# Where the constant part of an involution is added, and when a group norm takes its root

## The chip, the cores and the metric

The kernel runs on one core of a Trainium2 chip. A core has five engines with a queue of instructions each: TensorE (PE, matrix products; its weight loads are listed as PEld), VectorE (DVE), ScalarE (ACT), GpSimd (POOL) and SyncE (SP, which here issues most of the transfers). Each engine takes its own queue in order and waits on semaphores for the others. Products land in PSUM, eight banks of 2 KB per partition; all else lies in SBUF, 128 partitions wide. The metric is the time of one execution on the device, in microseconds. Before the change it is 2146.27 us, the median of three runs (2145.46 to 2147.59).

## The reference

The input `x` has 8 images, 256 channels and 56 x 56 pixels, in float32. Two layers follow each other, and the change concerns the first alone:

```python
    x = x + _L0_conv_ref(_gn(x), ...)     # layer 0: group norm, then an involution, added to x
    x = x + _L1_conv_ref(_gn(x), ...)     # layer 1: group norm, two ternary 3x3 convolutions with batch norms

    def _gn(v, G=32, eps=1e-5):
        ...
        return ((g - m) / jnp.sqrt(s + eps)).reshape(v.shape)

    def _L0_conv_ref(x, w_reduce, b_reduce, w_span, b_span):
        ker = einsum('bchw,oc->bohw', x, w_reduce) + b_reduce      # 256 -> 64 channels
        ker = einsum('bchw,oc->bohw', ker, w_span) + b_span        # 64 -> 16 groups x 49 taps
        ...
        out = (ker * patches).sum(axis=3)                          # 7x7 patches, a kernel of its own at each pixel
```

The involution makes a 7 x 7 kernel for each pixel and each of 16 groups of channels, and sums the pixel's neighbourhood with it.

## The kernel before

The program has three stages: the involution (to about 1060 us), the two convolutions, and the final sums. Only the first is changed.

**Tiling.** An image's 256 channels are taken as 4 quarters of 64 (`NCQ`, index `c`). A tile `xs[b, c]` holds one quarter of image `b`: partitions 0 to 63 the upper half of the picture, 64 to 127 the lower half, 28 rows of 56 pixels each. Each half is cut into patches of 3 x 8 pixels: 10 rows of patches (`ty`; the last has one pixel row only), 7 patches across.

**The norm is folded in.** The group norm is one scale and one shift per channel. The products use `x` as it is: the reduction's weights are scaled (`wrn`), and the sum is scaled when it is read out. What the shift adds to the involution is, per pixel, the shift times the sum of the 49 taps. This is the *constant part*.

**One row of patches**, `(b, c, ty)`, goes through these steps:

- `apply_row` (L872): 56 short products on TensorE (28 in the last row, L889) of a loaded neighbourhood `q` with the kernel matrices `a`, into a PSUM tile `pa`, of which there are two.
- `pick_out` (L893): ScalarE reads `pa` times a scale into `inv` (L899), VectorE adds the other channel groups of `pa` to it (L901), GpSimd adds `inv` to `x` (L906). In the very last quarter VectorE makes that last addition.
- `surround`, with `fill_rim` (L788, GpSimd) and `fill_end` (L801, ScalarE): they add the norm's mean at the rims of a neighbourhood that was loaded ahead.
- `generate` (L840), for the *next* quarter: 14 units. In each, TensorE makes the kernels (L857) into a pair of PSUM banks, ScalarE copies one bank with its bias into `a` (L861), VectorE the other (L865). Six banks go round between the units, the reductions and the constant part. `PER_ROW` says how many units belong to each row.
- `constant` (L810) is the last two steps of `generate`, both in row `ty` = 8. TensorE multiplies the reduced channels with the summed taps (L823, four banks). ScalarE takes each bank times the shift, plus a bias, into a tile `add` (L831), and GpSimd adds `add` to `x` of the next quarter (L837). Columns are 504 three times and 56 once.
- `reduce` (L742) and L759 make the reduced channels of the next image, in rows 24 to 34.
- One step of the rounding of the convolutions' weights (L310 to L330, VectorE, tiles `piece_w`), in most rows.
- The statistics (L149, VectorE): of the finished `x`, and of the next image's `x`.

**The norm of the next image.** `params` (L659) is a generator; from row 20 of an image on (rows counted 0 to 39 over its four quarters) it is advanced twice a row: at the start of a row, after `apply_row`, and after `pick_out`. Between two advances it emits:

1. row 20, start: a product over groups (L156); row 20, second: its read-out and the squared differences (L160 to L165);
2. row 21, start: a second product (L168); row 21, second: the variance (L171), `rstd_of` as a whole: plus epsilon (L135, VectorE), root (L137, ScalarE), reciprocal and a Newton step (L139 to L145, VectorE); then the norm's scale and shift (L173, L174), the scaled weights (L666), the scales (L673) and `shift` (L675);
3. after three empty yields, row 23, start: a product of the shift with the reduction's weights (L681); row 23, second: its read-out (L684); row 24, start: products for the rims (L688) and their copy (L692).

`gn2_params` (L695) does steps 1 and 2 for the second layer's norm, in the last image.

**Order.** After every row `pin` (L948) ties each instruction to the one before it on its engine, so every engine's queue follows the text. A long wait at the head of a queue thus holds up everything that stands behind it in the text.

Of the kernel before, what the change touches and what calls it, by code (L numbers as in the profile page):

```python
# [8 lines left out]
F32 = mybir.dt.float32  # L9
F32R = mybir.dt.float32r  # L10
AF = mybir.ActivationFunctionType
ALU = mybir.AluOpType
# [5 lines left out]
P = 128  # L18
B, C, H, W = 8, 256, 56, 56
# [70 lines left out]
def involution_tri_block_kernel(  # L90
# [37 lines left out]
    gn2 = const_tile([P, B, CT, 2], "gn2")  # L128


    def rstd_of(var, eps, name):

        n = var.shape[1]
        ve = small.tile([P, n], F32, tag=f"rs_ve{n}", name=f"ve_{name}")
        nc.vector.tensor_scalar(ve, var, eps, None, ALU.add)  # L135
        sq = small.tile([P, n], F32, tag=f"rs_sq{n}", name=f"sq_{name}")
        nc.scalar.activation(sq, ve, AF.Sqrt)  # L137
        r0 = small.tile([P, n], F32, tag=f"rs_r0{n}", name=f"r0_{name}")
        nc.vector.reciprocal(r0, sq)  # L139
        e = small.tile([P, n], F32, tag=f"rs_e{n}", name=f"e_{name}")  # L140
        nc.vector.tensor_tensor(e, r0, ve, ALU.mult)
        nc.vector.tensor_tensor(e, e, r0, ALU.mult)
        nc.vector.tensor_scalar(e, e, -0.5, 1.5, ALU.mult, ALU.add)
        r = small.tile([P, n], F32, tag=f"rs_r{n}", name=f"r_{name}")
        nc.vector.tensor_tensor(r, r0, e, ALU.mult)  # L145
        return r

    def image_stats(st, xt, j):
        nc.vector.bn_stats(st[:, j, :], xt[:, j * NC:(j + 1) * NC])  # L149
# [1 line left out]
    def group_norm_params(mv, dst, psum_tile, name, means=None):  # L151


        n = mv.shape[1]
        ps = psum_tile(f"gnp_{name}")
        nc.tensor.matmul(ps[:, :2 * n], grp_sb, mv.rearrange("p n s -> p (n s)"),  # L156
                         start=True, stop=True)
        yield
        gm = small.tile([P, n, 2], F32, tag=f"gn_gm{n}", name=f"gm_{name}")
        nc.vector.tensor_copy(gm.rearrange("p n s -> p (n s)"), ps[:, :2 * n])  # L160
        if means is not None:
            means.append(gm)
        d = small.tile([P, n], F32, tag=f"gn_d{n}", name=f"d_{name}")
        nc.vector.tensor_tensor(d, mv[:, :, 0], gm[:, :, 0], ALU.subtract)
        nc.vector.tensor_tensor(d, d, d, ALU.mult)  # L165
        yield
        ps2 = psum_tile(f"gnp2_{name}")
        nc.tensor.matmul(ps2[:, :n], grp_sb, d, start=True, stop=True)  # L168
        yield
        var = small.tile([P, n], F32, tag=f"gn_var{n}", name=f"var_{name}")  # L170
        nc.vector.tensor_tensor(var, ps2[:, :n], gm[:, :, 1], ALU.add)  # L171
        rs = rstd_of(var, GN_EPS, name)
        nc.vector.tensor_copy(dst[:, :, 0], rs)  # L173
        nc.vector.scalar_tensor_tensor(dst[:, :, 1], gm[:, :, 0], -1.0, rs, ALU.mult, ALU.mult)  # L174

    def batch_norm_before(stats, pre):

# [438 lines left out]
    with ExitStack() as ph1:  # L616
# [42 lines left out]
        def params(b):  # L659
# [13 lines left out]
                nc.vector.tensor_scalar(scales[:, c], half_sb, dst[:, c, 0:1], None, ALU.mult)  # L673
            shift = small.tile([P, NCQ], F32, tag="gn1b", name=f"gn1b_{b}")
            nc.vector.tensor_tensor(shift, dst[:, :, 1], bsum, ALU.mult)  # L675
            for _ in range(3):
                yield
            ps = ps_one(f"br_{b}")
            for c in range(NCQ):
                for i in range(2):  # L680
# [129 lines left out]
        def constant(b, c):  # L810

            n = (TY - 1) * TX
            xv = xs[b, c][:, :(TY - 1) * PY * W].rearrange("p (t y w) -> p y t w", y=PY, w=W)
            scale, bias = prm[b][0][:, c, 1:2], prm[b][2][:, c:c + 1]
            for i0 in (0, 2):
                ps = ps_pair(f"ks_{b}_{c}_{i0}")
                add = work.tile([P, 2 * PX * n], F32, tag="add", name=f"add_{b}_{c}_{i0}")
                for i in range(2):
                    py = (i0 + i) % PY
                    k0, m = (0, n) if i0 + i < PY else (NT, TX)  # L820
                    rows = slice(i * CR, (i + 1) * CR)
                    for h in range(2):
                        nc.tensor.matmul(ps[i][h * CH:(h + 1) * CH, :PX * m], wsx[rows, c, :],  # L823
                                         kr[py][rows, :, k0 + h * m:k0 + (h + 1) * m],
                                         start=True, stop=True)
                for i in range(2):
                    py = i0 + i
                    m = n if py < PY else TX
                    v = add[:, i * PX * n:i * PX * n + PX * m].rearrange(
                        "p (t w) -> p t w", w=W)  # L830
                    nc.scalar.activation(  # L831
                        v.rearrange("p t (k x) -> p t k x", x=PX),
                        ps[i][:, :PX * m].rearrange("p (x t k) -> p t k x", x=PX, k=TX),
                        AF.Identity, bias=bias, scale=scale)
                    x_ = xv[:, py] if py < PY else xs[b, c][:, PY * (TY - 1) * W:].rearrange(
                        "p (t w) -> p t w", w=W)
                    nc.gpsimd.tensor_tensor(x_, x_, v, ALU.add)  # L837
                yield

        def generate(b, c, a):  # L840
# [52 lines left out]
        def pick_out(b, c, ty, ps, n, m):  # L893
# [2 lines left out]
            inv = work.tile([P, TX, NP], F32, tag="inv", bufs=3, name=f"inv_{b}_{c}_{ty}")  # L896
            iv = inv[:, :, :n]
            scale = prm[b][1][:, c, 2 * (m == GQ):]
            nc.scalar.activation(iv, parts[:, :, 0], AF.Copy, scale=scale[:, 0:1])  # L899
            for g in range(1, m):  # L900
                nc.vector.scalar_tensor_tensor(iv, parts[:, :, g], scale[:, g:g + 1], iv,  # L901
                                               ALU.mult, ALU.add)
# [325 lines left out]
```

## Time and profile before

| | |
|---|---|
| median of three runs | 2146.27 us |
| profiled execution | 2168.06 us, of it 2166.2 us from first to last instruction |
| mean granted TensorE clock | 0.912 |
| TensorE, VectorE, ScalarE, GpSimd busy | 81%, 81%, 66%, 27% of the span |
| L831, ScalarE, 96 times 504 and 32 times 56 columns | 778 and 412 ns each |
| L837, GpSimd, the same counts | 1265 and 303 ns each |
| L901, VectorE, from PSUM, 168 and 56 columns | 377 and 272 ns each |
| L865, VectorE, from PSUM, 504 columns | 678 ns each |
| L899, ScalarE, 168 columns | 429 ns each |
| wait of the root L137 for L135 | 19.6 us in 7 times, longest 4.1 |

How to read it: a line of the profile names the source line, the engine, the operation and its tiles. "Busy" is the time in which an engine worked; idle time counts only where it sits on the way to the end. Each wait is named by what ended it; "issue" means that the profile shows nothing that the instruction waited for. TensorE's clock can be granted in part only (1.00 is full speed).

### The profile page before, as it was taken

The numbers are of one execution on the slowest core, as the hardware profiler recorded it, in microseconds if no ns is written. First come the engines' busy times: TensorE is split into PE (matmuls) and PEld (weight loads), VectorE is DVE, ScalarE is ACT, GpSimd is POOL, SyncE is SP. The second block draws the span as 40 slices with busy tenths as digits, with TensorE's granted clock in tenths as the row PEclk, the third lists the DMA queues.
The fourth block names the chain that finished last, engine by engine and source line by source line (L and its number), as shares of the span: only waits on it lengthen the run. The fifth ranks groups of instructions, "written<-read, shape, count | busy, mean of one in ns | idle before, by whom it ended". The sixth has DMA issues, their size and how long they took to land.

```text
span 2166.2 us, 70733 instructions
## 1 busy us (share of the span) xinstructions
PE 1761.7 (81%) x29680; PEld 1635.1 (75%) x29680; DVE 1756.3 (81%) x3350; ACT 1436.3 (66%) x3557; POOL 582.5 (27%) x955
## 2 busy tenths in 40 slices
PE   4898888989889898988799999998999999960000
PEld 4777777877777787776699999998999999960000
DVE  5787868787787868777799999998999999984444
ACT  3877777777878777777557666664576666653343
POOL 0564555465556546555200000000000000000000
PEclk9999999999999999999899999999999999985555
DMA  5667767686766758666733333335233333369999
GB/s 184 211 186 224 215 203 233 171 262 195 254 202 210 239 166 255 184 198 201 265 122 135 130 129 123 121 121 178 106 129 130 122 124 127 123 267 426 430 431 395
DMA packets 156250, 440.05 MB, mean 203 GB/s; under 512 B 63775, under 2 KB 74013, under 8 KB 148509
## 3 DMA queue, kind: packets, MB, share of 16 engines
q1 hardware_dynamic: 150336, 405.50, 55.0%
q10 hardware_dynamic: 5596, 30.03, 3.3%
q8 instruction: 235, 3.85, 0.8%
q14 instruction: 83, 0.67, 0.1%
HBM read 323.28 MB, written 112.20 MB: 201 GB/s over the span
## 4 chain that ended last, share of the span: by engine, by line
PE 64%; DMA 10%; DVE 10%; issue 7%; POOL 4%; ACT 3%; SPq 0%; ACTq 0%; POOLq 0%; DVEq 0%
PE c L557 40%; PE pg L857 12%; PE pa L889 7%; PE pk L750 3%; DMA y1f<-y1d 3%; DMA out_y<-x1f 2%; POOL q L788 2%; DMA y2f<-y2d 2%; ACT a L861 2%; POOL x L906 1%; PE ks L823 1%; DVE inv L901 1%; DMA x1f<-x1d 1%; DVE x1f L1140 1%; DVE a L865 1%
## 5 line engine op out<-in xcount | busy, mean ns | idle before, releaser
L557 PE MATMUL c<-pl,wq 128*128 128x392 f32 x4608 | 857.1, 348 | 9.5 <-ACT pl L429 9.2
L557 PEld LDWEIGHTS c<-pl,wq 128*128 128x128 f32 x4608 | 855.2, 190 | 11.2 <-ACT pl L429 9.6
L861 ACT ACTIVATE a<-pg,bt 126x126 f32<-126x126 f32 (+1 forms) x2048 | 530.3, 459 | 115.3 <-PE pg L857 114.8
L857 PE MATMUL pg<-kr,wl 64*126 64x140 f32 (+1 forms) x6144 | 467.9, 296 | 44.1 <-ACT a L861 16.9
L857 PEld LDWEIGHTS pg<-kr,wl 64*126 64x126 f32 x6144 | 407.6, 199 | 70.7 <-issue 26.3
L889 PE MATMUL pa<-a,q 126*32 126x48 f32 x17024 | 290.8, 215 | 68.4 <-issue 56.4
L889 PEld LDWEIGHTS pa<-a,q 126*32 126x32 f32 x17024 | 242.0, 116 | 136.2 <-issue 89.8
L865 DVE TENSOR_TENSOR a<-pg,bt 126x504 f32<-126x504 f32 (+4 forms) x640 | 281.6, 480 | 58.8 <-PE pg L857 57.3
L906 POOL TENSOR_TENSOR x<-x,inv 128x168 f32<-128x168 f32 x310 | 161.5, 521 | 413.7 <-DVE inv L901 378.9
L901 DVE SCALAR_TENSOR_TENSOR inv<-pa,gn1s,inv 128x168 f32<-128x168 f32 (+1 forms) x384 | 134.0, 351 | 160.9 <-ACT inv L899 157.8
L406 ACT CAST pl<-r 128x812 fp32r<-128x812 f32 x190 | 160.8, 867 | 131.0 <-DVE r L401 121.7
L382 POOL MEMSET xp<- 128x116 f32 x32 | 6.3, 196 | 825.6 <-DVE a L401 825.6
L788 POOL TENSOR_TENSOR q<-q,sides 126x256 f32<-126x256 f32 (+1 forms) x320 | 225.3, 705 | 6.4 <-DMA q<-in_x_nb 6.3
L407 DVE TENSOR_TENSOR pl<-r,pl 128x812 fp32r<-128x812 f32 x190 | 184.8, 998 | 25.1 <-ACT pl L406 23.5
L487 ACT ACTIVATE dummy<-y,nc 128x1568 f32<-128x1568 f32 (+1 forms) x128 | 200.2, 1564 | 4.8 <-DVE y L577 3.5
L899 ACT ACTIVATE inv<-pa,gn1s 128x168 f32<-128x168 f32 x320 | 133.2, 418 | 69.8 <-PE pa L889 48.6
L149 DVE BATCH_NORM_STATS2 st<-x 128x6 f32<-128x392 f32 x256 | 137.9, 555 | 9.8 <-DMA x<-in_x 9.4
L837 POOL TENSOR_TENSOR x<-x,add 128x504 f32<-128x504 f32 (+1 forms) x128 | 127.2, 1024 | 25.4 <-ACT add L831 25.4
L1107 ACT ACTIVATE xp<-raw,bi_bn,sc_bn 128x392 f32<-128x392 f32 (+1 forms) x125 | 83.0, 721 | 60.3 <-DVE a L401 58.9
L1087 ACT ACTIVATE xp<-raw,gn 128x392 f32<-128x392 f32 (+1 forms) x125 | 83.1, 721 | 58.9 <-DVE a L401 58.9
L1138 DVE SCALAR_TENSOR_TENSOR y1f<-y2f,sc_bn,y1f 128x3136 f32<-128x3136 f32 (+2 forms) x20 | 56.6, 2831 | 63.1 <-DMA y2f<-y2d 53.0
L750 PE MATMUL pk<-x,wrn 64*128 64x168 f32 (+1 forms) x1152 | 101.1, 315 | 0.8 <-issue 0.8
(177 smaller groups left out, 1794.9 us busy)
## 6 DMA issues: line engine op xcount, KB each, us to landing
q<-in_x_nb SPq DMA_DIRECT2D x320, 448.0 KB, 4.1
raw<-x1d SPq DMA_DIRECT2D x32, 812.0 KB, 5.9
raw<-y1d SPq DMA_DIRECT2D x32, 812.0 KB, 6.6
x<-in_x SPq DMA_DIRECT2D x64, 392.0 KB, 5.2
x1d<-x SPq DMA_DIRECT2D x64, 392.0 KB, 5.1
y1d<-y SPq DMA_DIRECT2D x30, 784.0 KB, 3.7
y2d<-y SPq DMA_DIRECT2D x30, 784.0 KB, 3.4
y1f<-y1d SPq DMA_DIRECT2D x14, 1568.0 KB, 14.2
```

Of the source, the lines that this page charges most:

```text
L406: nc.scalar.copy(hi, r)
L407: nc.vector.tensor_tensor(lo, r, hi.bitcast(F32), ALU.subtract)
L487: nc.scalar.activation(dst, v, f, bias=shift[:, to:to + 1], accum_out=stats[:, to, j, n:n + 1])
L557: nc.tensor.matmul(ps[:, to, :NM], wq[k][:, t, dx, to * P:(to + 1) * P], part[:, t, :, dx:dx + W], start=(c == 0), stop=(c == last))
L750: nc.tensor.matmul(ps[h][:, :m * W], wrn[rows, c, :], src[rows, r0:r0 + (m - 1) * PY + 1:PY, :], start=(c == 0), stop=(c == NCQ - 1))
L788: nc.gpsimd.tensor_tensor(v, v, z, ALU.add)
L857: nc.tensor.matmul(dst, wl[rows, c, gp, o:o + NQ], kr[py][rows, px, :], start=True, stop=True)
L861: nc.scalar.activation(dst[:, g + 1, p0 + j], ps[1][:NQ, j * nt + t0:j * nt + t1], AF.Identity, bias=bt[:, c, g + 1, p0 + j:p0 + j + 1])
L865: nc.vector.tensor_tensor(dst[:, g, p0:p0 + n].rearrange("q p t -> q t p"), ps[0][:NQ, t0 * n:t1 * n].rearrange("q (t p) -> q t p", p=n), ...
L889: nc.tensor.matmul(ps[o:o + m, k * w:(k + 1) * w], q[:NQ, k, o:o + m], av[:, t + k, g * w:(g + 1) * w], start=True, stop=True)
L901: nc.vector.scalar_tensor_tensor(iv, parts[:, :, g], scale[:, g:g + 1], iv, ALU.mult, ALU.add)
L906: engine.tensor_tensor(xv, xv, iv.rearrange("p t (y x) -> p y t x", x=PX), ALU.add)
```

## The change

Two things are changed. The constant part is no longer read by ScalarE into `add` and added by GpSimd; VectorE does both in one instruction (`scalar_tensor_tensor`: PSUM times the shift, plus `x`, into `x`), and the tile `add` is gone. The bias that L831 added is now added by the activation of `pick_out` (L899), which becomes `Identity` with a bias where it was `Copy`. And `rstd_of` becomes a generator with a yield on either side of the root: for `params`, the variance stays in row 21's second advance, the root moves to the start of row 22, and all from the reciprocal on to row 22's second advance. Two of the three empty yields after it are taken away, so that L681 and what follows keep their places.

```diff
-    def rstd_of(var, eps, name):
+    def rstd_of(var, eps, name, rs):
         ...
         sq = small.tile([P, n], F32, tag=f"rs_sq{n}", name=f"sq_{name}")
+        yield
         nc.scalar.activation(sq, ve, AF.Sqrt)
+        yield
         ...
-        return r
+        rs.append(r)
@@ group_norm_params
-        rs = rstd_of(var, GN_EPS, name)
-        nc.vector.tensor_copy(dst[:, :, 0], rs)
-        nc.vector.scalar_tensor_tensor(dst[:, :, 1], gm[:, :, 0], -1.0, rs, ALU.mult, ALU.mult)
+        rs = []
+        yield from rstd_of(var, GN_EPS, name, rs)
+        nc.vector.tensor_copy(dst[:, :, 0], rs[0])
+        nc.vector.scalar_tensor_tensor(dst[:, :, 1], gm[:, :, 0], -1.0, rs[0], ALU.mult, ALU.mult)
@@ params
-            for _ in range(3):
-                yield
+            yield
@@ constant
-            scale, bias = prm[b][0][:, c, 1:2], prm[b][2][:, c:c + 1]
...
-                add = work.tile([P, 2 * PX * n], F32, tag="add", name=f"add_{b}_{c}_{i0}")
...
-                    v = add[:, i * PX * n:i * PX * n + PX * m].rearrange(
-                        "p (t w) -> p t w", w=W)
-                    nc.scalar.activation(
-                        v.rearrange("p t (k x) -> p t k x", x=PX),
-                        ps[i][:, :PX * m].rearrange("p (x t k) -> p t k x", x=PX, k=TX),
-                        AF.Identity, bias=bias, scale=scale)
                     x_ = xv[:, py] if py < PY else xs[b, c][:, PY * (TY - 1) * W:].rearrange(
                         "p (t w) -> p t w", w=W)
-                    nc.gpsimd.tensor_tensor(x_, x_, v, ALU.add)
+                    x_ = x_.rearrange("p t (k x) -> p t k x", x=PX)
+                    nc.vector.scalar_tensor_tensor(
+                        x_, ps[i][:, :PX * m].rearrange("p (x t k) -> p t k x", x=PX, k=TX),
+                        prm[b][0][:, c, 1:2], x_, ALU.mult, ALU.add)
@@ pick_out
-            nc.scalar.activation(iv, parts[:, :, 0], AF.Copy, scale=scale[:, 0:1])
+            nc.scalar.activation(iv, parts[:, :, 0], AF.Identity, bias=prm[b][2][:, c:c + 1],
+                                 scale=scale[:, 0:1])
```

## The prediction

> **What bounds the kernel now.** I read the page's totals first, then the waits between 60 and 1060 us, where the changed code runs, then two stretches of the timeline. The page:
>
> ```profile
> PE 1761.7 (81%) x29680; PEld 1635.1 (75%) x29680; DVE 1756.3 (81%) x3350; ACT 1436.3 (66%) x3557; POOL 582.5 (27%) x955
> ...
> L837 POOL TENSOR_TENSOR x<-x,add 128x504 f32<-128x504 f32 (+1 forms) x128 | 127.2, 1024 | 25.4 <-ACT add L831 25.4
> ```
>
> TensorE leads, VectorE is next; the addition that leaves GpSimd is 127.2 us of work in the first stage. There TensorE is busy 88 of 100 us in the windows from 60 to 960, VectorE 75 to 82. So no more than TensorE's idle 12% can be won, and its waits say what of it this change reaches (waiting instruction, releaser: us, times, longest):
>
> ```profile
> PE pa L889 <- issue: 56.4, 53, 3.0
> PE pg L857 <- ACT a L861: 16.9, 16, 2.4
> PE pg L857 <- issue: 15.2, 12, 2.7
> PE pg L857 <- DVE a L865: 11.8, 9, 2.0
> PE pa L889 <- POOL q L788: 7.1, 7, 2.3
> ...
> PE pa L168 <- DVE d_a L165: 4.6, 5, 1.2
> ```
>
> 72 us have no visible releaser and aren't addressed. Numbering an image's 40 rows r = 0 to 39 by their first product, TensorE idles on average 1 us in r=1, 11 and 12, 2 us in r=22 and next to nothing from r=23 to 33, where it is the bound. The DVE waits lie in r=1, 11, 12, as in this stretch of image 1 (start, us, engine, line; in brackets the idle time before):
>
> ```profile
> 184.22 4.07 POOL L837 TENSOR_TENSOR x<-x,add 128x504 f32<-128x504 f32 x4
> 184.46 1.13 DVE L318 TENSOR_SCALAR piece_w<-piece_w 128x48 f32<-128x48 f32 x1
> ...
> 186.81 1.29 DVE L327 TENSOR_TENSOR piece_w<-piece_w 128x48 f32<-128x48 f32 x1
> ...
> 190.32 1.07 PE L857 MATMUL pg<-kr,wl 64*126 64x140 f32 x12 [2.02 <-DVE a L865]
> ```
>
> Two 48-column steps of the weight rounding take over 1.1 us each while GpSimd adds the constant part; by line, min/median/max in ns:
>
> ```profile
> L320 DVE TENSOR_TENSOR piece_w<-piece_w x64: 194/207/1147, 93.9 to 1014.9; 128x48 f32<-128x48 f32 x64
> L865 DVE TENSOR_TENSOR a<-pg,bt x620: 165/560/684, 64.5 to 1034.4; 126x378 f32<-126x378 f32 x62, 126x504 f32<-126x504 f32 x62, 126x252 f32<-126x252 f32 x31
> ```
>
> A step from SBUF stretches from 0.19 to 1.15 us beside a 1.25 us GpSimd addition; L865, which reads PSUM and one SBUF operand, never exceeds 0.68. The r=22 wait is the norm's root (image 4):
>
> ```profile
> 625.94 1.17 DVE L165 TENSOR_TENSOR d_a<-d_a 128x4 f32<-128x4 f32 x1
> 631.29 0.54 DVE L135 TENSOR_SCALAR ve_a<-var_a 128x4 f32<-128x4 f32 x1
> 631.86 0.21 ACT L137 ACTIVATE sq_a<-ve_a 128x4 f32<-128x4 f32 x1 [3.81 <-DVE ve_a L135]
> 632.97 0.83 PE L857 MATMUL pg<-kr,wl 64*126 64x140 f32 x2 [2.06 <-ACT a L861]
> 633.86 0.16 DVE L174 SCALAR_TENSOR_TENSOR gn<-gm_a,r_a 128x4 f32<-128x4 f32 x1
> 636.73 1.02 PE L681 MATMUL pa<-gn,wr 64*64 64x1 f32 x16
> ```
>
> ScalarE stands 3.81 us at the root, behind it the activations that free TensorE's PSUM banks.
>
> [...] The windows view gives 0.58 as the granted clock from 630.8 to 643.0, right after the stall at r=22[...].
>
> **The change part by part.**
>
> *Constant part, 32 times.* Removed: on ScalarE three L831 of 778 ns and one of 412, 2.75 us; on GpSimd three L837 of 1265 and one of 303, 4.1 us. Added on VectorE: three 504-column and one 56-column operation from PSUM with one SBUF operand. Not in the trace in this form; nearest rows are L865 at 504 columns (678 ns) and L901 at 56 (272): 3 x 0.678 + 0.272 = 2.31 us, or 2.2 with the overlap of neighbours. Bounds: 1.9 (L865 starts are 0.59 apart) and 3.0 (half more, should the strided PSUM read cost VectorE something; L831, with the same read, shows no such cost: 350 ns for 336 columns more than L899). I take 2.2: 70 us more on VectorE in all. The bias moves into L899: same instruction, no data, Copy to Identity with a bias column; L831 was Identity with bias already and fits L899's time per column, so 0.
>
> What hides the 2.2 us. From r=24 on VectorE idles 1 to 2.5 us a row waiting for L899, so the constant at r=28 is free. Those at r=8, 18 and 38 meet a tight VectorE, but today it also waits there for L899 queued behind L831: 0.5 to 0.7 us in r=0, 10 and 20. And the blocking goes: charging what each DVE operation takes over its form's fastest to the GpSimd instruction it ended with, L837 cost VectorE 32 us, per image 1.2 us in r=0-1, 1.0 in r=9-11, 1.26 in r=20-21. So VectorE's net lag there is 2.2 - 0.6 - 1.15 = about 0.4 us on average, and negative exactly where TensorE waited. Replaying image 1: constant to 185.0, rounding unblocked to 186.3, L901 of row 9 to 187.2 (0.45 us later than L889 wants its bank), L865 from 188.1 instead of 189.53: the 2.02 us wait shrinks to some 0.5. I count 9 of the 11.8 us (r=1, 11, 12) as won, and 4 of the 7.1 us behind L788, since GpSimd's next side additions no longer queue behind 4.1 us of L837 (in the last quarter alone one such wait was 2.3).
>
> *Norm's root, 7 times in a row's flow.* The root goes ahead of row 22's L899, behind all of row 21's L861 (2.2 us), so ScalarE's wait falls from 1.6-4.1 us to at most 2. But reciprocal to shift (16 small VectorE operations) move behind row 21's L865 and row 22's L901, and L681 on TensorE needs L174 half a row later. In image 4: 631.83 (L135 ends) + 1.97 (what is queued first) + 1.9 (L139 to L174 as today) = 635.7 instead of TensorE's 636.73. So the wait moves to L681, and only the difference is won; over the seven images 0.4, 0.5, 0.9, 0, 1.0, 1.0, 1.0 = 4.8 us. Behind L681 stand row 23's products and all of TensorE's queue. The two yields removed keep L681, L684 and the rim in their rows; no DMA moves. The constant at r=18 sits ahead of this chain and delays L657 and so L156, by up to 2.2 us; until L165 it is given back (1.26 blocking, 1.1 VectorE idle in r=18-20), so I count 0 at L681.
>
> *Clock.* Four half-clock stretches (17 us together) follow the waits of r=1 and 11 that go; at half rate they cost up to 8.5. I take 3, since other engines hold the pace there. After r=22 the stall ahead of L681 remains about 3 us long, so I expect half clock there as before: 0.
>
> *Against it.* Late banks behind the constants, as the 0.45 us above, -2[...].
>
> Sum: 9 + 4 + 4.8 + 3 - 5 = 16 us. The profiled execution took 2168.06 us (span 2166.2 and 1.9 around it): 2152 after. The median of the unprofiled runs is 22 us lower, most likely the profiling itself; the same 16 us from 2146.27 give 2130.
>
> **Rivals.**
> *The clock recovers.* If TensorE at r=22-24 no longer falls to half clock (some 10 us in images 4 to 6, 3 to 7 in the others, about 47 in all; half of 44 usable, 20), the time is 2110. For: clock 0.58 just after the stall. Against: the wait at L681.
> *No change.* The freed time is taken up by the 72 us of "issue" waits, which need no releaser, and by TensorE-bound rows 23 to 36: 2144. For: half of TensorE's idle is of that kind. Against: the DVE waits are separate gaps.
> *Slower: VectorE becomes the bound at r=0-1, 9-12 and 18-22.* Each 1 us of net lag at the three tight constants costs 3 x 7 = 21 us. With 0.4 counted as mostly harmless, it decides from 1.0 us, where the gains of 21 us are gone; at 1.6, if blocking by L788 and L906 merely takes L837's place, it is +13: 2159. For: VectorE at 89% in r=0-22. Against: GpSimd then idles in these rows.
> *The root's wait doesn't go* (L135 itself late): then 4.8 us less, 2135, inside the main case.
>
> **Chances.** Main case 0.55 (own range 2118 to 2141), clock 0.18, no change 0.13, slower 0.14. A measurement tells about 0.2%, 4.3 us, from no change. Faster 0.73, same 0.13, slower 0.14. The range 2108 to 2153 holds main, no change and most of the clock case, with the constant at 3.0 us.
>
> **What would show it.** L837 and L831 gone; a new DVE line of about 0.68 us at 504 columns, unaffected by GpSimd; L318, L320, L327 and L165 without values above 0.9; PE pg <- DVE a below 4 us; ACT sq <- DVE ve below 10 (19.6 now); a new PE wait at L681 for DVE gn. Wrong if the new line takes over 1 us, if PE waits at L156 and L889 for DVE exceed 20 us, or if half-clock stretches multiply.

## The result, and the profile after

The changed kernel takes 2147.89 us (median of 14 runs, 2142.24 to 2157.80), the kernel before, run beside it, 2148.11 us (14 runs, 2145.33 to 2160.39). The ratio is 1.0001 with a 95% interval of 0.9982 to 1.0020: no change. The forecast was 16 us faster.

The profiled execution after spans 2144.1 us, against 2166.2 us in the profile that the prediction read. That is no gain: a second profiled execution of the unchanged kernel spans 2141.8 us (the run c_before below), and of the 209 executions of it that ran beside the experiments, on five chips, the fastest took 2132.8 us, the slowest 2169.7. The first profile had caught a long one, with 126 us of half-clock stretches (TensorE's clock granted at 0.5) in the first stage where the second has 89. So "after" is set against the second profile from here on. "The stage" below runs from the first to the last row's products.

The page's totals after (engine, busy time, share of the span, instructions), the larger of its two queues of the kind "instruction" (packets, MB, share of the 16 DMA engines' time), and the pick-out's activation:

```profile
PE 1739.0 (81%) x29680; PEld 1615.3 (75%) x29680; DVE 1785.9 (83%) x3478; ACT 1388.8 (65%) x3429; POOL 457.2 (21%) x827
...
q8 instruction: 235, 3.85, 0.8%
...
L896 ACT ACTIVATE inv<-pa,gn1b,gn1s 128x168 f32<-128x168 f32 x320 | 162.1, 507 | 141.3 <-PE pa L886 104.4
```

The new line after at 504 columns, and the pick-out's activation in the second profile of before (busy us, mean ns):

```profile
L832 DVE SCALAR_TENSOR_TENSOR x<-ks,gn,x 128x504 f32<-128x504 f32 x96 | 65.1, 733 | 1.8 <-PE ks L823 1.7
```

```profile
L899 ACT ACTIVATE inv<-pa,gn1s 128x168 f32<-128x168 f32 x320 | 135.2, 424 | 58.1 <-PE pa L889 37.9
```

Against the second profile of before GpSimd lost 126 us of work, ScalarE 46, and VectorE gained 31: 71.0 us for the new line with its 56-column calls, less some 40, of which the prediction had charged 32 to the blocking by the old additions. The pick-out's activation takes 507 ns on average where it took 424. Two lines of VectorE in the second profile of before (shortest, median, longest in ns):

```profile
L327 DVE TENSOR_TENSOR piece_w<-piece_w x64: 195/493/1304, 96.1 to 998.3; 128x48 f32<-128x48 f32 x64
L165 DVE TENSOR_TENSOR d_a<-d_a x8: 162/400/1187, 27.3 to 868.7; 128x4 f32<-128x4 f32 x8
```

and after, with the new line:

```profile
L832 DVE SCALAR_TENSOR_TENSOR x<-ks,gn,x x128: 260/732/744, 59.8 to 1016.3; 128x504 f32<-128x504 f32 x96, 128x56 f32<-128x56 f32 x32
L330 DVE TENSOR_TENSOR piece_w<-piece_w x64: 196/374/902, 95.7 to 997.0; 128x48 f32<-128x48 f32 x64
L167 DVE TENSOR_TENSOR d_a<-d_a x8: 161/648/656, 26.5 to 869.1; 128x4 f32<-128x4 f32 x8
```

L832 is the constant part: 0.73 us at 504 columns, never longer than 0.744, with a GpSimd instruction beside 85 of those 96. L330 is the old L327, L167 the old L165: their longest fell, but the median of L167 rose from 0.40 to 0.65 us. GpSimd's shorter additions still go with such stretches: in the timeline of image 6, L144 takes 0.65 us from 876.82 on and ends with GpSimd's addition L790, 0.72 us from 876.72 on.

TensorE's waits from 60 to 1040 us, before (second profile):

```profile
PE pa L889 <- issue: 46.3, 50, 4.0
PE pg L857 <- ACT a L861: 16.7, 16, 2.4
PE pg L857 <- issue: 15.5, 12, 3.2
PE pg L857 <- DVE a L865: 11.5, 10, 2.1
PE pa L889 <- POOL q L788: 10.2, 9, 2.0
PE pa L168 <- DVE d_a L165: 5.4, 6, 1.2
PE pa L156 <- DVE mv L657: 3.7, 3, 1.5
```

and after:

```profile
PE pa L886 <- issue: 57.1, 51, 4.2
PE pg L854 <- issue: 20.1, 16, 3.5
PE pa L683 <- DVE gn L177: 12.4, 7, 2.6
PE pa L158 <- DVE mv L660: 11.5, 7, 2.1
PE pg L854 <- DVE a L862: 7.7, 13, 1.6
PE pa L886 <- DVE inv L899: 4.0, 5, 1.3
PE pa L886 <- DVE piece_w L329: 2.8, 4, 1.3
...
PE pa L886 <- POOL q L790: 0.7, 2, 0.4
```

The waits that the change aimed at are gone: the 16.7 us behind the root, the 10.2 behind GpSimd's rim additions, a third of the 11.5 behind `a`. In their place stand 12.4 us at L683 (the old L681), 11.5 at L158 (the old L156, 3.7 then), and 77 us of "issue" where there were 62. Over the whole stage TensorE's idle time was 118 us before and is 126 after. The second profile of the changed kernel (c_after) has 8.8 us at L683, 12.1 at L158 and 122 in all, so a few us of such a sum are chance.

Rows 18 to 23 of image 6 after show the two new waits (start, us, engine, line; in brackets the idle time before):

```profile
864.22 2.22 DVE L832 SCALAR_TENSOR_TENSOR x<-ks,gn,x 128x504 f32<-128x504 f32 x4
...
866.35 0.56 DVE L151 BATCH_NORM_STATS2 st<-x 128x6 f32<-128x392 f32 x1
866.94 0.26 DVE L660 BATCH_NORM_AGGREGATE mv<-st 128x2 f32<-128x24 f32 x1
...
867.26 0.39 PE L158 MATMUL pa<-mv,grp_sb 128*128 128x8 f32 x2 [1.14 <-DVE mv L660]
...
873.13 0.54 DVE L135 TENSOR_SCALAR ve_a<-var_a 128x4 f32<-128x4 f32 x1
...
873.70 0.20 ACT L138 ACTIVATE sq_a<-ve_a 128x4 f32<-128x4 f32 x1
...
876.07 0.16 DVE L141 RECIPROCAL r_a<-sq_a 128x4 f32<-128x4 f32 x1
...
877.98 0.15 DVE L177 SCALAR_TENSOR_TENSOR gn<-gm_a,r_a 128x4 f32<-128x4 f32 x1
878.19 1.02 PE L683 MATMUL pa<-gn,wr 64*64 64x1 f32 x16 [1.84 <-DVE gn L177]
```

The constant part of row 18 takes VectorE for 2.22 us; behind it stands the last piece of the next image's statistics, and TensorE waits at L158 for what is made from that. The root itself no longer stops ScalarE, but 2.2 us of queued VectorE work lie between L138 and L141. TensorE now waits at L683.

### The profile page after: what moved, and what is told of

It is laid out like the page before. It is cut to its first block, busy times and chain, and to the rows that moved or that the text cites. A ratio compares the mean times of both kernels' runs of the same rounds, so it can differ in the third digit from the quotient of the medians.

```text
span 2144.1 us, 70526 instructions
## 1 busy us (share of the span) xinstructions
PE 1739.0 (81%) x29680; PEld 1615.3 (75%) x29680; DVE 1785.9 (83%) x3478; ACT 1388.8 (65%) x3429; POOL 457.2 (21%) x827
## 3 DMA queue, kind: packets, MB, share of 16 engines
q1 hardware_dynamic: 150336, 405.50, 55.5%
## 4 chain that ended last, share of the span: by engine, by line
PE 65%; DVE 13%; DMA 10%; issue 6%; ACT 3%; POOL 2%; SPq 0%; ACTq 0%; POOLq 0%; DVEq 0%
PE c L560 40%; PE pg L854 13%; PE pa L886 7%; PE pk L752 4%; DMA x1f<-x1d 2%; DMA y1f<-y1d 2%; DVE a L862 2%; DMA out_y<-x1f 2%; DMA y2f<-y2d 2%; DVE x L832 2%; ACT a L858 2%; DVE st L151 2%; DVE inv L899 1%; DVE x1f L1138 1%; PE ks L823 1%
## 5 line engine op out<-in xcount | busy, mean ns | idle before, releaser
L854 PE MATMUL pg<-kr,wl 64*126 64x140 f32 (+1 forms) x6144 | 451.4, 291 | 30.1 <-issue 20.1
L854 PEld LDWEIGHTS pg<-kr,wl 64*126 64x126 f32 x6144 | 394.0, 193 | 55.2 <-issue 26.0
L886 PE MATMUL pa<-a,q 126*32 126x48 f32 x17024 | 287.9, 214 | 69.5 <-issue 57.1
L886 PEld LDWEIGHTS pa<-a,q 126*32 126x32 f32 x17024 | 239.7, 115 | 136.2 <-issue 94.2
L896 ACT ACTIVATE inv<-pa,gn1b,gn1s 128x168 f32<-128x168 f32 x320 | 162.1, 507 | 141.3 <-PE pa L886 104.4
L899 DVE SCALAR_TENSOR_TENSOR inv<-pa,gn1s,inv 128x168 f32<-128x168 f32 (+1 forms) x384 | 134.4, 351 | 129.3 <-ACT inv L896 119.8
L790 POOL TENSOR_TENSOR q<-q,sides 126x256 f32<-126x256 f32 (+1 forms) x320 | 225.3, 704 | 7.2 <-DMA q<-in_x_nb 7.1
L151 DVE BATCH_NORM_STATS2 st<-x 128x6 f32<-128x392 f32 x256 | 138.2, 556 | 10.2 <-DMA x<-in_x 10.2
L1138 DVE TENSOR_TENSOR x1f<-x1f,y1f 128x3136 f32<-128x3136 f32 (+2 forms) x20 | 55.3, 2772 | 51.1 <-DMA out_y<-x1f 31.8
## 6 DMA issues: line engine op xcount, KB each, us to landing
y1f<-y1d SPq DMA_DIRECT2D x14, 1568.0 KB, 14.3
```

What stands on the lines that cost most here:

```text
L790: nc.gpsimd.tensor_tensor(v, v, z, ALU.add)
L854: nc.tensor.matmul(dst, wl[rows, c, gp, o:o + NQ], kr[py][rows, px, :], start=True, stop=True)
L886: nc.tensor.matmul(ps[o:o + m, k * w:(k + 1) * w], q[:NQ, k, o:o + m], av[:, t + k, g * w:(g + 1) * w], start=True, stop=True)
L896: nc.scalar.activation(iv, parts[:, :, 0], AF.Identity, bias=prm[b][2][:, c:c + 1], scale=scale[:, 0:1])
```

## The experiments

Before the runs, these were the theories; the expectations, quoted as they were put on record, number them. The first suspicion was the order around row 18: the constant part sits there ahead of the norm's last statistics, and L683 comes too early after the moved root. Theory 1 in its narrow form says that this row alone eats the gain. Against it stood the price of the bias, and plain chance in the clock. Theory 4, formed later: VectorE sets the pace at all three tight constants, in rows 8, 18 and 38. Theory 5: whatever wait is removed comes back as "issue" or in rows that TensorE bounds. A number not explained here is explained in the expectation that uses it.

All results, each as a ratio to the kernel before on the same chip, with its 95% interval. The median of before lay between 2145 and 2156 us from chip to chip, so only the ratios compare:

| run | edit | median us | ratio |
|---|---|---|---|
| c_before | none | 2145.55 | 0.9997 [0.9973, 1.0021] |
| c_after | the change | 2144.55 | 1.0001 [0.9984, 1.0018] |
| c_root | the root's yields alone | 2139.21 | 0.9966 [0.9952, 0.9980] |
| c_const | constant part and bias alone | 2144.25 | 0.9996 [0.9975, 1.0017] |
| d_early_mv | change, last statistics a row earlier | 2141.27 | 0.9975 [0.9960, 0.9989] |
| d_late_l683 | change, L683 a row later | 2143.97 | 0.9987 [0.9967, 1.0007] |
| d_both | change, both of these | 2135.65 | 0.9945 [0.9926, 0.9964] |
| f_both_again | the same once more | 2144.91 | 0.9965 [0.9949, 0.9980] |
| d_no_bias | change, bias left out | 2143.71 | 0.9988 [0.9975, 1.0001] |
| f_old18 | change, row 18's constant as before | 2150.37 | 0.9986 [0.9971, 1.0000] |
| f_new18 | change, only row 18's constant on VectorE | 2149.20 | 0.9978 [0.9962, 0.9993] |
| f_root_order | root and both orders, constant as before | 2143.27 | 0.9960 [0.9942, 0.9978] |
| g_dup18 | change, constant twice in row 18 | 2174.58 | 1.0086 [1.0070, 1.0103] |
| g_dup_rest | change, constant twice in rows 8, 28, 38 | 2187.05 | 1.0151 [1.0131, 1.0172] |
| g_before_half | before, half of each `q` load | 2127.29 | 0.9873 [0.9853, 0.9893] |
| g_after_half | change, half of each `q` load | 2120.80 | 0.9843 [0.9822, 0.9863] |
| i_new_quant | d_both, rounding steps in other rows | 2140.63 | 0.9949 [0.9918, 0.9979] |
| i_old_quant | f_root_order, the same move | 2135.64 | 0.9930 [0.9902, 0.9958] |

Where TensorE stood idle in images 0 to 6, by rows, us over the seven images, in brackets the part that is "issue" (added up from the traces):

| rows | c_before | after | d_both | i_new_quant | i_old_quant |
|---|---|---|---|---|---|
| 0-1 | 6.5 (1.8) | 3.9 (0.8) | 4.0 (0.4) | 4.2 (2.9) | 2.4 (2.3) |
| 2-7 | 22.6 (20.1) | 29.3 (27.8) | 30.2 (27.2) | 25.7 (23.4) | 34.7 (28.0) |
| 8-13 | 20.2 (6.6) | 17.8 (4.3) | 16.3 (6.2) | 10.0 (9.0) | 10.9 (9.0) |
| 14-19 | 19.4 (19.2) | 19.6 (19.5) | 20.9 (16.7) | 22.3 (22.3) | 19.8 (19.8) |
| 20-23 | 24.2 (0.4) | 27.7 (1.9) | 14.3 (3.3) | 12.1 (9.6) | 9.5 (5.7) |
| 24-39 | 5.5 (5.5) | 7.6 (7.6) | 12.0 (8.6) | 14.5 (14.0) | 20.0 (19.8) |
| sum | 98.4 (53.7) | 105.9 (61.9) | 97.7 (62.2) | 88.8 (81.2) | 97.4 (84.6) |

### The two parts alone

c_root keeps L831 and L837 and has only the new `rstd_of`; c_const has only the new constant part and the bias. c_before and c_after are the two kernels themselves.

> The kernel before once more, for a second profile of it. If the profile on which the prediction was made (span 2166 us) was a slow one of its kind, this one lies near the median, 2140 to 2155 us, with fewer half-clock stretches than 136 us between 60 and 1060 us, and nearly the same waits by releaser: PE pg for ACT a about 17 us, PE pg for DVE a about 12, PE L156 for DVE mv about 5. If the change really freed 20 us that something gave back, the span is again near 2166.

> The changed kernel beside the others on the same chip: ratio 0.998 to 1.002. PE's waits again sit at L683 for DVE gn (about 12 us) and at L158 for DVE mv (about 11).

> Only the root moves; the constant part stays with ScalarE and GpSimd. Theory 1 (the wait only changes its place: VectorE's chain up to the norm's scale sets when L683 can run): PE pg for ACT a falls from about 17 to below 4 us, and a new wait of PE at L683 for DVE gn of 8 to 14 us stands in its place; ratio 0.997 to 1.000. Theory 2 (the root is a clear gain and the constant part on VectorE loses it again): the new wait is below 5 us and the ratio is 0.990 to 0.995.

> Only the constant part moves to VectorE, with its bias in the pick-out; the root stays as before. Theory 1: PE pg for ACT a stays at 13 to 18 us, PE at L156 for DVE mv rises from about 5 to about 11 us, PE pg for DVE a and PE pa for POOL q fall by 8 us together: ratio 0.998 to 1.002. Theory 2: the waits for VectorE outweigh what is won, ratio 1.004 to 1.010.

The root alone makes the kernel 0.34% faster, 7.3 us (4 to 10), the constant part alone changes nothing (0.9996), and both together change nothing either: the parts do not add.

Two waits of c_const, and one of c_root:

```profile
PE pa L156 <- DVE mv L657: 11.0, 7, 2.1
...
PE pg L852 <- ACT a L856: 9.2, 10, 1.7
```

```profile
PE pa L683 <- DVE gn L177: 10.8, 6, 2.6
```

In c_root the wait behind the root is gone and L683 waits 10.8 us; in c_const the wait behind the root had already fallen from 16.7 to 9.2 us, while L156 waits 11.0 us. The constant part thus brings a wait at the start of row 20. Whether it is this wait that eats what the root gives, the next two sections ask. Why the root alone wins 7 us is not to be read in the rows: its profile has 25.7 us of idle time in rows 20 to 23, before has 24.2.

### The order around row 18, and the bias

d_early_mv puts the last piece of the statistics ahead of row 18's constant part; d_late_l683 leaves the three empty yields, so that L683 comes a row later; d_both does both:

```diff
-                if more and 4 <= r < 20:
+                if more and 4 <= r < 19:
                     gn1_stats(b + 1, (r - 4) // NCB, (r - 4) % NCB)
+                    if r == 18:
+                        gn1_stats(b + 1, NCQ - 1, NCB - 1)
@@ params
-            yield
+            for _ in range(3):
+                yield
```

> The changed kernel, with the last piece of the next image's statistics (one L151 and the L660 behind it) put into row 18, ahead of the constant part on VectorE, in place of row 19. Theory 1 (the constant part at r=18 delays the norm's chain and eats what the root wins): PE at L158 for DVE mv falls from about 12 us to below 5, the ratio to before is 0.996 to 0.999. Theory 2 (VectorE's total work is what counts, so its order does not matter): the wait turns up again at L170 or L683, ratio 0.999 to 1.002.

> The changed kernel with the two empty yields kept, so that the product L683 comes one row later, at the start of row 24, and its read-out and the rim products a row later too. Theory 1 (L683's wait for the norm's scale gives back what the root won): PE at L683 for DVE gn falls from 9 to 12 us to below 2, ratio 0.995 to 0.998. Theory 2: TensorE is held by the same VectorE chain anyway and waits for DVE a or DVE inv instead, ratio 0.999 to 1.002.

> Both moves of order together. Theory 1: their gains add, PE waits at L158 and L683 below 6 us together (now about 21), ratio 0.991 to 0.996. Theory 2: ratio 0.998 to 1.001.

> The changed kernel with both moves of order once more, beside the one above: ratio to before 0.992 to 0.997.

The first takes the wait at L158 away (in its trace the wait of L170 rises to 6.6 us), the second that at L683. Alone they give 0.25% and 0.13%, the second within its interval of nothing; together 0.55% and, run again, 0.35%. Rows 20 to 23 lose half of their idle time, 27.7 to 14.3 us. But of the 13.4 us freed there the sum keeps 8: rows 24 to 39 take 4.4 back. In the profile of f_both_again the sum is 4 us below the change's. With the order mended the changed kernel is 7 to 12 us faster than the one before, still less than the forecast 16.

d_no_bias leaves the bias out of the sum and goes back to `Copy`:

```diff
-            nc.scalar.activation(iv, parts[:, :, 0], AF.Identity, bias=prm[b][2][:, c:c + 1],
-                                 scale=scale[:, 0:1])
+            nc.scalar.activation(iv, parts[:, :, 0], AF.Copy, scale=scale[:, 0:1])
```

> The changed kernel with Copy and no bias in the pick-out, as it was before; the bias of the constant part is left out altogether. L896 took 507 ns in place of L899's 418, 28 us more on ScalarE in all. Theory 1 (ScalarE is not what paces): L896 is back at about 418 ns and the ratio stays at 0.997 to 1.001. Theory 3 (each row's way from product to pick-out runs through ScalarE, and the 89 ns are what the change loses): ratio 0.988 to 0.995.

The pick-out's activation by line, after:

```profile
L896 ACT ACTIVATE inv<-pa,gn1b,gn1s x320: 397/492/720, 61.5 to 1037.0; 128x168 f32<-128x168 f32 x160
```

and without the bias:

```profile
L896 ACT ACTIVATE inv<-pa,gn1s x320: 307/402/594, 63.1 to 1038.3; 128x168 f32<-128x168 f32 x160
```

The bias costs 90 ns a time, 29 us of ScalarE over 320. In the time it is 0.9988 against 1.0001, some 3 us with the intervals overlapping: not told from nothing.

### Is it row 18 alone?

In f_old18 row 18's constant part goes back to ScalarE and GpSimd, in f_new18 all the others do; the branch is `if c == 2` or `if c != 2` in `constant`, and the bias stays in the pick-out. f_root_order has the root's yields and both orders, with the constant part as before.

> The changed kernel, but the constant part of quarter c=2 (made at r=18) is read by ScalarE and added by GpSimd as before (its bias still in the pick-out); the other three quarters stay with VectorE. Theory 1 (only the constant at r=18, ahead of the next image's statistics, eats the root's gain): PE at L158 for DVE mv falls below 6 us, ratio 0.996 to 0.999. Theory 4 (the constant part costs as much at r=8 and r=38): ratio 0.9985 to 1.001.

> The reverse: only the constant part of quarter c=2 is with VectorE, the other three are with ScalarE and GpSimd as before. Theory 1: all of the loss and little of the gain are here, PE at L158 for DVE mv 10 to 13 us, ratio 0.999 to 1.003. Theory 4: one quarter of the loss, ratio 0.9965 to 0.9985, near that of the root alone (0.9966).

> The root alone with both moves of order (statistics in row 18, L683 a row later); the constant part stays with ScalarE and GpSimd. If the constant part on VectorE is worth something once its place is mended, this is 1 to 4 us slower than the version with both, ratio to before 0.995 to 0.997; if it is worth nothing, the two are equal, 0.993 to 0.996.

Both splits come out within 0.1% of each other (0.9986 and 0.9978), although the wait at L158 is 3.1 us in one and 11.0 in the other. Theory 1 in its narrow form is not borne out (it asked for 0.999 to 1.003 in f_new18): the wait at L158 doesn't carry the time by itself. And with the order mended no difference shows between the places of the constant part: 0.9960 with it as before, 0.9945 and 0.9965 with it on VectorE. The intervals leave room for some 4 us.

### What a microsecond of VectorE costs

g_dup18 and g_dup_rest compute the constant part a second time into a tile that nobody reads, in row 18 alone, or in rows 8, 28 and 38:

```diff
+                    if c == 2:
+                        again = work.tile([P, PX * n], F32, tag="again", bufs=1, name=f"again_{b}_{c}_{py}")
+                        nc.vector.scalar_tensor_tensor(
+                            again[:, :PX * m].rearrange("p (t k x) -> p t k x", k=TX, x=PX),
+                            ps[i][:, :PX * m].rearrange("p (x t k) -> p t k x", x=PX, k=TX),
+                            prm[b][0][:, c, 1:2], x_, ALU.mult, ALU.add)
```

> The changed kernel with VectorE's constant part of quarter c=2 (at r=18) made twice, once into a tile that nobody reads: 2.4 us more on VectorE in 8 places. Theory 1 (there every us of VectorE is paid for): PE at L158 for DVE mv rises from 12 to 20 us or more, ratio 1.004 to 1.009. If VectorE's place doesn't matter: below 1.002.

> The same doubling in the other three quarters (r=8, 28, 38) and not at r=18: 2.4 us more on VectorE in 24 places, 58 us in all. Theory 1 (free at r=28, nearly free at r=8 and 38 once GpSimd no longer blocks): ratio 1.000 to 1.004. Theory 4 (the constant part on VectorE costs as much at r=8 and 38 as at 18): ratio 1.008 to 1.018.

The added work and the wait that grew, from the groups and the waits of g_dup18:

```profile
L834 DVE SCALAR_TENSOR_TENSOR again<-ks,gn,x 128x504 f32<-128x504 f32 (+1 forms) x32 | 19.7, 617 | 0.1
```

```profile
PE pa L158 <- DVE mv L660: 30.6, 7, 4.7
```

19.7 us of VectorE were added in row 18 and the kernel became (1.0086 - 1.0001) x 2148 = 18.3 us slower than the change: 93% is paid (the two intervals allow 70 to 120%). In the other rows 59.3 us were added and 32.2 paid. Idle time rose in rows 0 and 1 from 3.9 to 16.7 us and in rows 8 to 13 from 17.8 to 25.3. If row 28's share, 19.8 us, is free, as the prediction held (VectorE waits there), 82% of the rest is paid. So theory 4 holds in this direction: VectorE has no room in rows 8 to 11, 18 to 23, and 38 to 1. Waiting is only part of the price. In these profiles TensorE is idle 138 and 140 us of the stage, 12 and 14 more than after, but its half-clock stretches are 133 and 146 us where after, on another chip, has 85 (more on this below, under the clock).

### What fills the freed time

g_before_half and g_after_half load only the first half of the columns of each neighbourhood `q` (224 KB in place of 448) from the second quarter on, into five fixed tiles; the products then use what an earlier load left in the other half. All instructions of the engines stay.

```diff
-            q = qpool.tile([P, TX, P], F32, tag="q", name=f"q_{b}_{c}_{ty}")
+            q = qs[((b * NCQ + c) * TY + ty) % NQB]
+            f = TX * P if (b, c) == (0, 0) else TX * P // 2
-                              x_nb[b, c, (HQ - QY - PY * ty) * QX:(HQ - QY - PY * ty) * QX + P, :])
+                              x_nb[b, c, (HQ - QY - PY * ty) * QX:(HQ - QY - PY * ty) * QX + P, :f])
```

> The kernel before, with half of each neighbourhood load left out (the second half of q's columns keeps what an earlier load left there), in five fixed tiles: 224 KB in place of 448 KB for each of the 310 later rows. It takes traffic away and no instruction of TensorE. Theory 5 (TensorE's waits without a releaser are waits for its own instructions, which come by transfers that share the engines with the loads): PE's issue waits in the first stage fall from 64 to 73 us to below 40, the time falls by 10 to 30 us, ratio 0.986 to 0.995. Theory 6 (they have nothing to do with transfers): issue waits stay above 60 us.

> The changed kernel with the same half of the loads left out. Theory 5 (what the change freed was taken up by waits for instructions): with these gone the change shows: 6 to 12 us faster than the kernel before with half loads, that is a ratio to before 0.003 to 0.006 below that one's. Theory 1 alone (the wait for VectorE's chain ate it, whatever the transfers do): no difference between the two beyond 0.002.

Without a single instruction less on any engine both became faster, by 1.3 and 1.6%, though hardly any wait names a load. "Issue" over the stage fell from 64 to 52 us before and from 78 to 53 after. From 60 to 1040 us g_before_half has

```profile
PE pa L890 <- issue: 40.0, 46, 4.8
...
PE pg L858 <- issue: 11.2, 14, 1.9
```

and g_after_half

```profile
PE pa L887 <- issue: 42.0, 45, 4.3
...
PE pg L855 <- issue: 10.2, 9, 2.1
```

The trace says where: the queue q8, of the kind "instruction", brings packets of 16 KB, 235 in all, about one each 5 us in this stage. They took 0.8% of the 16 DMA engines' time, those of q1, which carries the loads, 55.5% (after; q1 falls from 405.5 to 334.4 MB in g_after_half). In the second profile of before, 35 of the 64 us of "issue" lie in gaps within which such a packet landed, after 45 of 78; with half the loads 16 and 18. TensorE resumes a median 1.34 us after the landing before, 1.44 after, and after the change eight in ten of these lags lie between 1.25 and 1.51 us.

That q8 brings TensorE's own instructions is an estimate from these lags; no trace names the engine that it serves. Most of its packets leave no such gap: of the 194 in this stage 17 land in one before and 18 after, but these gaps hold the 35 and 45 us. The late packets are those that travel when the transfers are dense: after the change, the 16 DMA engines were busy with other transfers for 0.92 of the time that the 18 late packets took, and 0.55 for the other 176. With the halved loads only 8 are late. The packets' own time is the same (median 0.96 us late, 0.98 otherwise), so the estimate is that they are held up before they start; where, no run shows. The rest of "issue", in whose gaps nothing lands, stays unexplained. So does part of the gain: 27 and 34 us were won, while "issue" fell by 12 and 25 in profiles from different chips.

The change is worth 0.3% with half the loads (0.9873 to 0.9843), 6.5 us, where it is worth nothing with all; the intervals, from four executions each, overlap a little, so this points to these packets and doesn't prove it. Theory 5 had asked for less "issue" than the 52 us measured, so it is upheld in kind only.

### Giving VectorE room

If VectorE holds the pace in the tight rows, taking work from it there should give time back. The rounding steps of the convolutions' weights can go anywhere. Here they are moved, two a row into rows 24 to 37, and none remain in rows 0, 1, 8 to 11, 18 to 23, 38 and 39:

```diff
                 if m * TY + ty >= QUANT_AT:
-                    next(quant, None)
+                    for _ in range(2 if 24 <= r < 38 else r % 20 in (2, 3, 4, 5, 6, 7, 12, 13, 14, 15, 16, 17)
+                                   and r < 20):
+                        next(quant, None)
```

> The change with both moves of order (last statistics before the constant part of row 18, L683 a row later), and the rounding steps of the weights given to other rows: two a row in rows 24 to 37, one in rows 2 to 7 and 12 to 17, none in rows 0, 1, 8 to 11, 18 to 23, 38 and 39. All of the work is still done. Some 14 steps of about 0.75 us, 10 us of VectorE per image, leave the rows around the constant parts for those in which VectorE waits. Theory 4 (VectorE sets the pace around rows 8, 18 and 38, nearly 1 to 1): at half of that price or more, 30 to 65 us over the seven images with rounding steps, ratio 0.970 to 0.988, and PE waits for DVE in rows 0, 1, 10 to 12 and 20 to 22 nearly gone. Theory 5 (what VectorE frees comes back as issue waits or in the rows that TensorE bounds): ratio 0.992 to 0.998, issue waits above 85 us in the first stage. A third outcome, the doubled steps wait for their transfers at SP and hold VectorE in rows 24 to 37: waits of PE for DVE a there, ratio above 0.998.

> The same move of the rounding steps with the constant part left as before (root in a yield of its own, both moves of order). It tells what the constant part on VectorE is worth once VectorE has room. Theory 4: now VectorE has the time, the banks of the constant part come free sooner and ScalarE is relieved, so this kernel is slower than the one above by 4 to 11 us, ratio higher by 0.002 to 0.005. Theory 5: the two are within 0.001, as before (0.996 and 0.9955).

TensorE's waits of i_new_quant, 60 to 1040 us:

```profile
PE pa L887 <- issue: 73.6, 69, 3.9
PE pg L855 <- issue: 22.7, 15, 4.0
PE pa L887 <- DVE inv L900: 5.3, 7, 2.3
PE pa L158 <- DVE mv L942: 3.0, 1, 3.0
```

The waits for other engines are all but gone: 13 us over the stage, 48 after the change, 54 before. "Issue" is 100 us. The ratios, 0.9949 and 0.9930, are those of the mended order alone within their intervals. The predicted 30 to 65 us are not there. Theory 5 had asked for 0.992 to 0.998 and more than 85 us of "issue", and both came. 60 of the 100 us now lie in gaps with a landing packet of q8: more than half of this "issue" goes with these packets. And i_old_quant, with the constant part on ScalarE and GpSimd, is no slower than i_new_quant: no gain from the place of the constant part shows even when VectorE has room.

i_old_quant is the lowest ratio with all work done. It is faster than the kernel before by 0.7% (0.4 to 1.0), and d_both by 0.35 to 0.55; between these two the intervals don't decide.

## Why the prediction was wrong, point by point

**"I count 9 of the 11.8 us as won, and 4 of the 7.1": this step failed, and with it the sum.** The prediction took the waits that the constant part's move removes for time won. The waits behind GpSimd's rim additions and behind `a` did shrink, by 9.5 and 3.8 us, but the time did not follow. The constant part alone gives 0.9996 (0.9975 to 1.0017), about 1 us where 13 were counted, less 5 against it. With the order mended it gives nothing that the runs can tell. What stood in the place of the waits comes in the points on L681 and on "issue". The prediction's own sign of being wrong was there: TensorE's waits for VectorE at L158 and L886 (the old L156 and L889) are 23 us together, where it had named 20.

**The new instruction: right.** 2.2 us for the four were forecast, 2.22 stand in the timeline. Beside GpSimd its longest is 0.744 us, alone 0.743, and the longest stretches beside the old additions are gone (L330's longest 0.90 where it was 1.30; L167's 0.66 where it was 1.19).

**The bias at 0: wrong.** It is 90 ns: the activation's median is 402 ns without it (d_no_bias) and 492 with it (after). Most of that can be estimated from the profile of before. L831's own two forms, 778 ns at 504 columns and 412 at 56, give 0.82 ns a column, 275 ns for the 336 columns by which it exceeds L899; the difference to L899 was 350 ns. The other 75 fit the bias column; the prediction took them for columns. The effect on the time stayed below what the runs can tell.

**The root: right in kind, in size perhaps by luck.** The forecast moved the wait to L681 and counted 4.8 us as won; the wait behind the root fell by 14.8 us and 12.4 came at L683. Alone the root gives 7.3 us (4 to 10), but its profile doesn't show them in the rows in which the 4.8 were counted.

**"I count 0 at L681" for row 18's constant part: this step failed too.** The prediction saw that L657, and with it L156, would come up to 2.2 us late, and followed the delay along VectorE, where it is given back. But TensorE takes its queue in order too and stops at L156 itself: 11.5 us where it was 3.7. It does so in every profile with the constant part on VectorE ahead of the last statistics (10.4 to 12.8 us with full loads and the constant part made once). Rows 20 to 23, for which the prediction had a gain, have 27.7 us of idle time where they had 24.2; the second profile of the change has some 23. In time this wait alone is worth little: without it the change gains 0.15% (f_old18) or 0.25% (d_early_mv), 3 to 5 us, the first with an interval that reaches nothing. Both moves of order together brought 0.35 to 0.55%, 7 to 12 us.

**"Issue", 3 of the 5 us against the change: too small, as far as single profiles tell.** Over the stage it is 64, 73, 59 and 80 us without the new constant part (c_before, the first profile, c_root, f_root_order). With it, it is 69 to 88 in eight profiles (after, c_after, c_const, and the runs on order and bias), 79 on average. That is +10, but the two groups overlap, and two profiles of the same kernel differ by 9 (before) or 13 (d_both and its repeat). The 9.5 us won behind GpSimd's rim additions, more than the 4 forecast, stood half in rows 2 and 12 of images 0 to 6; rows 2 to 7 have 6.7 us more idle time than before, and more than that is "issue" (20.1 to 27.8).

**The waits behind `a` in rows 1, 11 and 12: half.** 9 us were counted. Rows 0, 1 and 8 to 13 went from 26.7 to 21.7, since waits behind `inv` and `piece_w`, 4.9 us more than before, stand where those behind `a` had been.

**The clock at +3: nothing to see, and its working was rough.** Half-clock stretches in the stage: 89 us before, 85 and 95 in the two profiles after. The half clock that the prediction put right after the stall at r=22 of image 4 began at 632.77 us, before the stall ended at 632.97. The twenty traces together show more. In the stage every half-clock stretch is a multiple of 3.41 us long, and starts on a grid of 3.41 us that is fixed within its trace. Of 371 full-clock windows of this grid in which TensorE was idle for 1.6 us or more, 322 were followed by half clock; of 4784 with less idle time, 75. By these counts idle time costs more where it is gathered in one window.

How much the clock weighs: over the twenty profiles TensorE's busy time in the stage grows by some 0.37 us for each us of half clock (839 us at 59, 874 at 146). And the kernels that gained had the higher mean clock in their runs: 0.919 for c_root, 0.922 and 0.924 for d_both and its repeat, beside 0.916 to 0.918 for the kernel before on the same chips. Among those executions of before, 0.001 of clock goes with about 1 us. By this estimate some 3 of the root's 7 us, and 4 to 7 of those of the mended order, go with the clock. It is no proof of the way: the change itself has 0.918 beside 0.916, and no gain.

**The base: wrong.** The 22 us between profile and median were put down to the profiling. The second profile, at 2143.66 us, lies below the median; it was one long execution.

**The rivals.** "No change" came true with a chance of 0.13. The mechanism it named, "issue" taking the freed time, had a part in it as far as the profiles tell, together with the wait at L158. "Slower" had the right slope: it said 21 us for each microsecond of lag at the tight constants (3 x 7), and the doubled constants give 0.82 to 0.93 of that. Only, as far as the time tells, the lag wasn't there. "The clock recovers" didn't happen. The range held the time.

What stays open: where the root's gain lies beyond what the clock gives, how the lost 13 us divide between the wait at L158, "issue" and the clock, and what the part of "issue" is in which no packet lands.

## What to carry to other kernels

Two limits can lie at nearly the same height: here VectorE's time was paid at 0.8 to 0.9 when added, and gave almost nothing when taken away, while TensorE's "issue" stood at 100 us of the stage (i_new_quant) where it was 78 (after). Before counting a removed wait as won, ask what TensorE would do in that gap if nothing released it late; where "issue" is half of its idle time, price the gain at half or less. And when work is put into an in-order queue, follow the delay first to the nearest instruction behind it for which another in-order engine waits, not to the end of its own engine's chain.

## What the runs showed of the hardware

- Halving the loads of `q`, which hardly any wait names, made the kernel 1.3 to 1.6% faster (g_before_half, g_after_half). In the profile after, 18 of the 194 packets of 16 KB on the queue of the kind "instruction" landed in gaps of TensorE, of up to 4.2 us, for which no releaser is shown; the DMA engines were 0.92 busy with other transfers while these travelled, 0.55 while the others did. TensorE resumed a median 1.44 us after the landing.
- In the twenty traces TensorE's clock was half after 322 of 371 full-clock windows of 3.41 us in which it was idle for 1.6 us or more, and after 75 of 4784 with less; it never stayed full after more than 1.85 us.
- The same kernel's half-clock stretches in one stage were 126 us in one execution and 89 in another; its executions spread over 2132.8 to 2169.7 us, so one profile says little about 1%.
- Replacing `Copy` by `Identity` with a bias column took the pick-out's activation, of 168 or 56 columns, from a median 402 to 492 ns (d_no_bias, after).
